# A conditional residual adapter: another order of the opening

## The chip, the cores and the metric

The kernel runs on one core of a Trainium2 chip. The metric is the time of one execution on the device in microseconds. The core has five engines that run side by side, each with its own queue of instructions in program order: TensorE (matmul, PE), VectorE (DVE), ScalarE (ACT), GpSimd (POOL) and SyncE (SP), which here only issues DMAs. Waits between them are semaphores.

## The reference

For each of 128 batches of 128x512 floats an id from 0 to 8 picks one of ten adapters and one of ten rows of gamma, beta and b2:

```python
w1 = W1[language_ids]            # (512, 128) of each batch
w2 = W2[language_ids]            # (128, 512)
h = relu(einsum('bsh,bha->bsa', hidden_states, w1) + b1[language_ids][:, None, :])
adapted = einsum('bsa,bah->bsh', h, w2) + b2[language_ids][:, None, :]
x = hidden_states + adapted
mean = mean(x, axis=-1, keepdims=True)
var = mean(square(x - mean), axis=-1, keepdims=True)
normed = (x - mean) * rsqrt(var + 1e-05)
out = hidden_states + normed * gamma[language_ids][:, None, :] + beta[language_ids][:, None, :]
```

All of it is in float32.

## The kernel before

**Steady work of a batch.** TensorE transposes x in four 128x128 pieces (`transpose_x`, L235), ScalarE copies the result out of PSUM (`copy_xT`, L239), TensorE multiplies by W1 (`down`, L258), ScalarE applies relu and b1 (`relu`, L266), TensorE multiplies by W2 (`up`, L275) into one of five PSUM buffers. VectorE adds the residual and sums the rows (`residual`, L292), ScalarE squares (`square`, L315) and takes the root, VectorE scales by gamma (`scale`, L358) and adds the rest (`finish`, L367). GpSimd prepares two operands ahead of that: x + b2 (`add_b2`, L245) and x + beta (`add_beta`, L252), the latter straight into the output tile. SP stores the outputs of two batches at a time (`store`, L371) from a ring of five output tiles. The loop over `i` works on several batches at once: transposes of batch `i`, `down` of `i - 1`, `up` of `i - 2`, the normalization of `b = i - 3`. The order on every engine is the order in the code; `keep` ties each instruction to the one before it on its engine.

**Where b2 is added.** On GpSimd for most batches. For some, VectorE adds it in PSUM (`b2_by_vector`, L285). For a few, TensorE adds it by one more matmul, a "pick" (`b2_by_matmul`, L274). The choice spreads the load over the three engines.

**The opening.** Gamma, beta and b2 must stand in all 128 partitions, since every batch reads a row by its id. The ten rows of each are loaded into one tile `rows`, split into three bfloat16 parts (L184 to L188), and each of the 30 rows is spread by a matmul with a column of `pick` (`spread`, L206); ScalarE or VectorE copies it out (L209, L211). These 30 turns are interleaved by hand with the transposes and projections of batches 0 to 3. A few matmuls on ones come before (`spin`, L486).

**W1.** The first `FIRST` = 9 batches load their W1 by id from DRAM (`load_first`, L154); each such tile is one of five buffers, so from the sixth on the load waits for the `down` five batches before. Later batches copy it on ScalarE (`stage_w1`, L226) out of one of two resident copies: `w1e` below `EARLY` = 21, in a layout whose x is transposed by strided columns, and `w1` from there on, loaded by four DMAs at i = 8, 10, 12, 14.

**SP's queue** is in the order of the code, too: a DMA whose buffer isn't free holds all behind it. x comes in groups of four batches in four buffers; the loads of the first three groups are split in halves.

Of the kernel before, what the change touches and what calls it, by code (L numbers as in the profile page):

```python
# [8 lines left out]
FP = mybir.dt.float32  # L9
# [7 lines left out]
P = 128  # L17
G = 4
EPS = 1e-5
FIRST = 9  # L20
EARLY = 21
LATE = 12
U = 2

# [2 lines left out]
def cond_resid_kernel(ctx: ExitStack, tc: tile.TileContext, x, itok, W1, b1, W2, b2, gamma, beta, out):  # L27
# [63 lines left out]
    keep(nc.sync.dma_start(out=ids, in_=itok.rearrange("(o b) -> o b", o=1)))  # L91
# [7 lines left out]
    keep(nc.vector.memset(warm, 1.0))  # L99
    keep(nc.scalar.activation(warm, warm, AF.Abs_reciprocal_sqrt))  # L100
    def load_w1(k):
        keep(
            nc.sync.dma_start(out=w1[:, :, k, :], in_=W1[:, k * P : (k + 1) * P, :].rearrange("l p a -> p l a"))
        )

    ident = const.tile([P, P], FP, name="ident")
    make_identity(nc, ident)
    eps = const.tile([P, 1], FP, name="eps")
    nc.gpsimd.memset(eps, EPS)
    ones = const.tile([P, P], BF, name="ones")  # L110
    nc.gpsimd.memset(ones, 1.0)

    R = 3 * L
# [6 lines left out]
    keep(nc.vector.tensor_scalar(pick[:, L : 2 * L], pick[:, L : 2 * L], -0.5, None, ALU.mult))  # L122

    lids, w1s = {}, {}

# [57 lines left out]
    left = rp.tile([P, H], FP, tag="r", name="left")  # L183
    keep(nc.vector.tensor_copy(parts[0:R, :], rows[0:R, :]))  # L184
    keep(nc.vector.tensor_tensor(left[32 : 32 + R, :], rows[0:R, :], parts[0:R, :], ALU.subtract))
    keep(nc.vector.tensor_copy(parts[32 : 32 + R, :], left[32 : 32 + R, :]))
    keep(nc.vector.tensor_tensor(left[64 : 64 + R, :], left[32 : 32 + R, :], parts[32 : 32 + R, :], ALU.subtract))
    keep(nc.vector.tensor_copy(parts[64 : 64 + R, :], left[64 : 64 + R, :]))  # L188

    b1T = const.tile([P, L], FP, name="b1T")  # L190

# [8 lines left out]
    b2_b = const.tile([P, L * H], FP, name="b2_b")  # L200

    def spread(r, copier):
        t = (beta_b, gamma_b, b2_b)[r // L]
        row = p_y.tile([P, H], FP, tag="y", name=f"row_{r}")
        pick_r = pick[:, r : r + 1].to_broadcast([96, P])
        keep(nc.tensor.matmul(row, lhsT=pick_r, rhs=parts[:96, :], start=True, stop=True))  # L206
        dst = t[:, r % L * H : (r % L + 1) * H]
        if copier is nc.scalar:
            keep(nc.scalar.copy(dst, row))  # L209
        else:  # L210
            keep(nc.vector.tensor_copy(dst, row))  # L211
# [56 lines left out]
    def up(b):  # L268
        v = lid(b, ET.PE)
        ys[b] = p_y.tile([P, H], FP, tag="y", name=f"py_{b}")  # L270
        m = b2_by_matmul(b)
        if m:
            pick_b = pick[:, bass.ds(v + 2 * L, 1)].to_broadcast([96, P])
            keep(nc.tensor.matmul(ys[b], lhsT=pick_b, rhs=parts[:96, :], start=True, stop=False))  # L274
        keep(nc.tensor.matmul(ys[b], lhsT=hT[b], rhs=w2[:, bass.ds(v * H, H)], start=not m, stop=True))  # L275
        del hT[b]
# [217 lines left out]

    def spread_turn(lo, hi):
        for r in range(lo, hi):
            spread(r, nc.scalar if r % 7 in (1, 3, 5) else nc.vector)

    def x_turn(b):
        transpose_x(b)  # L500
        copy_xT(b)

    x_turn(0)
    transpose_b1()
    spread_turn(0, 4)
    x_turn(1)
    spread_turn(4, 11)
    down(0)
    relu(0)
    spread_turn(11, 15)  # L510
    down(1)
    relu(1)
    x_turn(2)
    spread_turn(15, 19)
    x_turn(3)
    down(2)
    relu(2)
    spread_turn(19, 24)
    down(3)
    relu(3)  # L520
    spread_turn(24, R)
    up(0)
    up(1)

    for i in range(3, B + U):
        b = i - U - 1
        if b > G and b % G == 2 and b // G + 3 < NG:
            load_x(b // G + 3)
        if i == 5:
            load_x(3)  # L530
        if i in (8, 10, 12, 14):
            load_w1((i - 8) // 2)
        if i == 4:
            up(2)
        if i == 5:
            up(3)
        if i > 3 and on(i):
            transpose_x(i)
        if b <= E:
            add_b2(b + 2)  # L540
            add_beta(b)
        if i > 4 and on(i - 1):
            down(i - 1)
        if i > 3 and on(i):
            copy_xT(i)
        if b == 2:
            scalar_means(0)
            deviation(0)
        if i > 4 and on(i - 1):
            relu(i - 1)  # L550
        if i + 1 >= LATE and on(i + 1):
            stage_w1(i + 1)
        if i > 5 and on(i - U):
            up(i - U)


        g, half = divmod(b, 2)
        p = g - 1
        mine, old = 0 <= p < B // 2, 0 <= p - 1 < B // 2
        if b == E:  # L560
# [36 lines left out]

        for n, engine in ((i + 3, ET.Activation), (i - U + 3, ET.PE), (b + 1, ET.DVE), (b + 5, ET.Pool)):
            if on(n):
                lid(n, engine)  # L600

# [36 lines left out]
```

## Time and profile before

| what | value |
|---|---|
| time, median of 3 runs | 307.37 us (307.01 to 307.51) |
| the profiled execution | 307.08 us |
| its span, first to last instruction | 305.3 us |
| mean granted TensorE clock | 0.991 |
| busy: PE, DVE, ACT, POOL | 294.6, 295.5, 282.1, 283.7 us |
| DMA traffic | 77.85 MB, mean 255 GB/s |

"Busy" is the time in which an engine executes; registers, branches and DMA issues don't count. In the lines of a view "x8" is a number of instructions, and the time after "<-" in brackets is an idle time and what ended it. The chain of waits is followed back from the last instruction, at each step to what released it. A row of stages gives, in order, its length, the busy time of PE, PEld (weight loads), DVE, ACT and POOL with their instructions, the granted clock, the share of the DMA engines and GB/s.

### The profile page before, as it was taken

How to read it: one execution, taken by the hardware profiler on the slowest of the kernel's cores; microseconds unless marked ns; L12 is line 12 of the kernel's file. 1: busy time of each engine (PE TensorE's matmuls, PEld its weight loads, DVE VectorE, ACT ScalarE, POOL GpSimd, SP SyncE). 2: the span in 40 equal slices, each digit the busy share in tenths (PEclk: the TensorE clock that was granted, in tenths of full speed). 3: DMA queues.
4: the chain of work that ended last, by engine and by line, in shares of the span. 5: the costliest groups of instructions: out<-in, count | busy, mean ns of one | idle time of the engine just before them, and what ended most of it. 6: DMA issues, size and time to landing. Idle time of an engine off the chain costs nothing.

```text
span 305.3 us, 6987 instructions
## 1 busy us (share of the span) xinstructions
PE 294.6 (97%) x1836; PEld 220.2 (72%) x1836; DVE 295.5 (97%) x770; ACT 282.1 (92%) x777; POOL 283.7 (93%) x239
## 2 busy tenths in 40 slices
PE   8999999999999999999999999999999999999980
PEld 3748787777777777777777777777777777777740
DVE  6889999999999999999999999999999999999995
ACT  3758999999999999999999999999999999999982
POOL 1349898999999999999999999999999999999995
PEclk9999999999999999999999999999999999999996
DMA  6999999966678667766877666778766767782244
GB/s 234 393 386 387 373 370 355 375 226 251 212 273 273 232 200 232 244 254 224 275 247 235 223 210 251 254 241 275 258 196 221 237 240 235 275 276 105 112 166 172
DMA packets 44057, 77.85 MB, mean 255 GB/s; under 512 B 1993, under 2 KB 7892, under 8 KB 44018
## 3 DMA queue, kind: packets, MB, share of 16 engines
q1 hardware_dynamic: 43382, 76.84, 72.8%
q10 hardware_dynamic: 636, 0.57, 0.6%
q8 instruction: 15, 0.25, 0.3%
q14 instruction: 24, 0.20, 0.2%
HBM read 43.85 MB, written 33.55 MB: 253 GB/s over the span
## 4 chain that ended last, share of the span: by engine, by line
PE 92%; DVE 5%; issue 1%; ACT 1%; DVEq 0%; POOL 0%; ACTq 0%; POOLq 0%
PE ph L258 36%; PE py L275 34%; PE pxT L235 18%; PE row L206 2%; DVE py L358 2%; PE idle L486 1%; DVE py L292 1%; DVE o L367 1%; DVE b_b L211 0%; ACT n L414 0%; ACT sq L315 0%; ACT sq L400 0%; DVE o L425 0%; ACT w1s L226 0%; DVE rstd L334 0%
## 5 line engine op out<-in xcount | busy, mean ns | idle before, releaser
L252 POOL TENSOR_TENSOR o<-x,beta_b 128x512 f32<-128x512 f32 x128 | 163.7, 1294 | 10.5 <-DVE beta_b L211 9.5
L258 PE MATMUL ph<-xT,w1s 128*128 128x128 f32 x1024 | 135.3, 275 | 0.0
L275 PE MATMUL py<-w,hT 128*128 x256 | 131.1, 595 | 0.5 <-DVE b_b L211 0.5
L245 POOL TENSOR_TENSOR r<-x,b_b 128x512 f32<-128x512 f32 x96 | 124.3, 1295 | 7.1 <-DVE b_b L211 6.2
L258 PEld LDWEIGHTS ph<-xT,w1s 128*128 128x128 f32 x1024 | 124.9, 192 | 1.0 <-ACT hT L266 0.5
L235 PEld LDWEIGHTS pxT<-ident,x 128*128 128x128 f32 x512 | 66.6, 151 | 65.3 <-issue 49.3
L358 DVE SCALAR_TENSOR_TENSOR py<-py,nmean,gamma_b 128x512 f32<-128x512 f32 x126 | 95.2, 755 | 0.2
L367 DVE SCALAR_TENSOR_TENSOR o<-py,rstd,o 128x512 f32<-128x512 f32 x122 | 91.4, 750 | 0.0
L315 ACT ACTIVATE sq<-py,sum 128x512 f32<-128x512 f32 x124 | 85.8, 692 | 2.8 <-DVE py L292 2.6
L235 PE MATMUL pxT<-ident,x 128*128 128x128 f32 x512 | 78.2, 276 | 0.0
L239 ACT COPY xT<-pxT 128x512 f32<-128x512 f32 x128 | 74.7, 583 | 3.6 <-PE pxT L235 3.6
L292 DVE SCALAR_TENSOR_TENSOR py<-py,r 128x512 f32<-128x512 f32 x96 | 66.6, 693 | 0.2
L226 ACT COPY w1s<-w 128x512 f32 x107 | 65.6, 613 | 0.0
L266 ACT ACTIVATE hT<-ph,b1T 128x128 f32<-128x128 f32 x128 | 46.9, 366 | 8.2 <-PE ph L258 2.9
L275 PEld LDWEIGHTS py<-w,hT 128*128 128x128 f32 x256 | 39.2, 192 | 2.7 <-issue 1.0
L315 ACT ACTIVATION_READ_ACCUMULATOR sq<-py,sum 128x1 f32 x124 | 25.1, 202 | 0.0
L292 DVE SCALAR_TENSOR_TENSOR py<-py,x 128x512 f32<-128x512 f32 x32 | 22.4, 699 | 0.4
L285 DVE TENSOR_TENSOR py<-py,b_b 128x512 f32<-128x512 f32 x29 | 20.2, 697 | 0.7 <-PE py L275 0.6
L325 ACT ACTIVATE root<-ssq,eps 128x2 f32<-128x2 f32 x62 | 16.4, 265 | 0.0
L292 DVE DVE_READ_ACCUMULATOR py<-py,r 128x1 f32 x96 | 13.8, 143 | 0.0
L306 ACT ACTIVATE nmean<-sum 128x2 f32<-128x2 f32 x62 | 12.3, 198 | 0.0
L329 DVE SCALAR_TENSOR_TENSOR part<-ssq,root 128x2 f32<-128x2 f32 x62 | 9.4, 152 | 0.2 <-ACT root L325 0.2
(55 smaller groups left out, 92.0 us busy)
## 6 DMA issues: line engine op xcount, KB each, us to landing
out_dram<-o SPq DMA_DIRECT2D x61, 512.0 KB, 3.4
x<-in_x_dram SPq DMA_DIRECT2D x29, 1024.0 KB, 6.6
x<-in_x_dram SPq DMA_DIRECT2D x6, 512.0 KB, 8.7
w1e<-in_L_cond_W_dram SPq DMA_DIRECT2D x2, 1280.0 KB, 12.4
w<-in_L_cond_W_dram SPq DMA_DIRECT2D x4, 640.0 KB, 8.0
w1s<-in_L_cond_W_dram SPq DMA_DIRECT2D x9, 256.0 KB, 8.1
w<-in_L_cond_W_dram SPq DMA_DIRECT2D x1, 1792.0 KB, 10.0
w<-in_L_cond_W_dram SPq DMA_DIRECT2D x1, 768.0 KB, 5.3
```

The lines of the kernel that those rows point to most:

```text
L226: keep(nc.scalar.copy(w1s[b].rearrange("p k a -> p (k a)"), src))
L235: keep(nc.tensor.transpose(pxs[b][:, k, :], cols, ident))
L239: keep(nc.scalar.copy(xT[b], pxs.pop(b)))
L245: keep(nc.gpsimd.tensor_tensor(rs[b], xb(b), b2_b[:, bass.ds(v * H, H)], ALU.add))
L252: keep(nc.gpsimd.tensor_tensor(os[g][:, j, :], xb(b), beta_b[:, bass.ds(v * H, H)], ALU.add))
L258: nc.tensor.matmul(phs[b], lhsT=w1s[b][:, k, :], rhs=xT[b][:, k, :], start=(k == 0), stop=(k == KC - 1))
L266: keep(nc.scalar.activation(hT[b], phs.pop(b), AF.Relu, bias=b1T[:, bass.ds(lid(b, ET.Activation), 1)]))
L275: keep(nc.tensor.matmul(ys[b], lhsT=hT[b], rhs=w2[:, bass.ds(v * H, H)], start=not m, stop=True))
L292: nc.vector.scalar_tensor_tensor(ys[b], ys[b], 1.0, r, ALU.mult, ALU.add, accum_out=col(sums, b))
L315: nc.scalar.activation(sq, ys[b], AF.Square, bias=col(sums, b), scale=-float(H), accum_out=col(ssqs, b))
L358: nc.vector.scalar_tensor_tensor(ys[b], ys[b], col(nmeans, b), gamma_b[:, bass.ds(v * H, H)], ALU.add, ALU.mult)
L367: nc.vector.scalar_tensor_tensor(o, ys.pop(b), rstds[g][:, j : j + 1], o, ALU.mult, ALU.add)
```

## The change

The opening is written anew.

- **Loads.** Gamma and b2 go to `rows`, b1 follows, and beta goes four times into a zeroed tile `beta_rows`, once at the head of each 32 partitions. x of batches 0, 1, 2 and 3 is loaded one batch at a time. W2 comes in halves of five, behind the W1 of batch 2. The fourth group of x (`x_3`) is loaded ahead of the loop.
- **Rows.** Only gamma and b2 are spread by picks (20 turns, R = 20). Beta's rows are spread by ten VectorE shuffles (`beta_row`). The three bfloat16 parts are made by two subtractions on VectorE and two copies on ScalarE, which read the upper halves of the floats.
- **b2** of batches 0 to 3, 14 and 18 is added by TensorE; batch 5's goes to GpSimd.
- **W1** is loaded by id for 12 batches instead of 9; `w1e` serves up to batch 29 instead of 20, and the loads of `w1` move to i = 16, 18, 20, 22.
- **Order.** Batch 3's transposes and `down` move behind the first `up`. `add_beta` runs two batches earlier in GpSimd's order, next to `add_b2` of the same batch. The spin loses a half matmul.

```diff
-FIRST = 9
-EARLY = 21
+FIRST = 12
+EARLY = 30
...
-    keep(nc.scalar.dma_start(out=rows[0:L, :], in_=beta))
-    keep(nc.sync.dma_start(out=rows[L : 2 * L, :], in_=gamma))
-    keep(nc.scalar.dma_start(out=rows[2 * L : 3 * L, :], in_=b2))
-    load_part(0, 2)
-    keep(nc.scalar.dma_start(out=b1r, in_=b1))
+    beta_rows = rp.tile([P, H], FP, tag="r", name="beta_rows")
+    keep(nc.vector.memset(beta_rows, 0.0))
...
+    def load_beta(q, engine):
+        keep(engine.dma_start(out=beta_rows[32 * q : 32 * q + L, :], in_=beta))
...
+    keep(nc.scalar.dma_start(out=rows[0:L, :], in_=gamma))
+    keep(nc.sync.dma_start(out=rows[L : 2 * L, :], in_=b2))
+    keep(nc.scalar.dma_start(out=b1r, in_=b1))
+    load_beta(0, nc.scalar)
+    load_beta(1, nc.sync)
+    load_beta(2, nc.scalar)
+    load_beta(3, nc.sync)
+    load_part(0, 1)
+    load_part(1, 2)
...
-    load_w2(0, 3)
     load_first(0)
     load_first(1)
-    load_part(2, G)
+    load_part(2, 3)
     load_first(2)
+    load_w2(0, 5)
+    load_w2(5, L)
+    load_part(3, G)
     load_first(3)
-    load_w2(3, L)
...
     load_part(2 * G, 2 * G + 2)
+    load_first(2 * G)
     load_early(0, 5)
-    load_first(2 * G)
+    load_first(2 * G + 1)
+    load_part(2 * G + 2, 3 * G)
+    load_first(2 * G + 2)
     load_early(5, L)
-    load_part(2 * G + 2, 3 * G)
+    load_first(2 * G + 3)
+    xs[3] = xp.tile([P, G, H], FP, tag="x", name="x_3")
+    load_part(3 * G, 3 * G + 2)
+    load_part(3 * G + 2, 4 * G)
...
+    keep(nc.vector.tensor_tensor(rows[32 : 32 + R, :], rows[0:R, :], upper(0), ALU.subtract))
+    keep(nc.scalar.copy(parts[0:R, :], upper(0)))
+    keep(nc.vector.tensor_tensor(parts[64 : 64 + R, :], rows[32 : 32 + R, :], upper(32), ALU.subtract))
+    keep(nc.scalar.copy(parts[32 : 32 + R, :], upper(32)))
...
-        return b in (5, B - 2, B - 1)
+        return b < 4 or b in (14, 18) or b >= B - 2
...
-        return b < 4 or 8 <= b < B - 8 and (b % 4 == 1 if b < 24 else b % 16 in (1, 6, 11) or b % 32 == 30)
+        return 8 <= b < B - 8 and (b % 4 == 1 if b < 24 else b % 16 in (1, 6, 11) or b % 32 == 30)
...
     spin(9, H)
-    spin(1, H // 2)
...
+    def beta_row(lo, hi):
+        for r in range(lo, hi):
+            keep(nc.vector.stream_shuffle(beta_b[:, r * H : (r + 1) * H], beta_rows, [r] * 32))
...
+    transpose_b1()
+    beta_row(0, 3)
     x_turn(0)
+    spread_by(S_, 0)
+    spread_by(V, 1)
+    spread_by(S_, 2)
+    spread_by(V, 3)
     x_turn(1)
     down(0)
     relu(0)
+    spread_by(S_, 4)
+    x_turn(2)
+    spread_by(S_, 5)
+    spread_by(V, 6)
     down(1)
     relu(1)
+    beta_row(3, 5)
...
     down(2)
     relu(2)
...
+    spread_by(V, 14)
+    beta_row(5, 7)
+    spread_by(S_, 15)
+    spread_by(S_, 16)
+    spread_by(S_, 17)
+    spread_by(V, 18)
+    spread_by(S_, 19)
+    up(0)
+    beta_row(7, 10)
+    add_beta(0)
+    add_beta(1)
+    add_beta(2)
+    add_beta(3)
+    x_turn(3)
+    up(1)
     down(3)
     relu(3)
...
-        if i in (8, 10, 12, 14):
-            load_w1((i - 8) // 2)
+        if i in (16, 18, 20, 22):
+            load_w1((i - 16) // 2)
...
             add_b2(b + 2)
-            add_beta(b)
+            if 4 <= b + 2 <= E:
+                add_beta(b + 2)
...
-        if 0 < g and b <= E and half == 1:
+        if 0 <= g and b <= E and half == 1:
             scalar_means(g)
             deviation(g)
```

More of the change, by code (lines that the diff above doesn't have):

```diff
@@ L104, in load_w1 @@
         )
+    ones = const.tile([P, P], BF, name="ones")
+    nc.gpsimd.memset(ones, 1.0)
     ident = const.tile([P, P], FP, name="ident")
@@ L109, in cond_resid_kernel @@
     nc.gpsimd.memset(eps, EPS)
-    ones = const.tile([P, P], BF, name="ones")
-    nc.gpsimd.memset(ones, 1.0)
-    R = 3 * L
+    R = 2 * L
     parts = const.tile([P, H], BF, name="parts")
@@ L121, in cond_resid_kernel @@
     keep(nc.vector.tensor_tensor(pick, both, ident[:96, 64 : 64 + R], ALU.add))
-    keep(nc.vector.tensor_scalar(pick[:, L : 2 * L], pick[:, L : 2 * L], -0.5, None, ALU.mult))
+    keep(nc.vector.tensor_scalar(pick[:, 0:L], pick[:, 0:L], -0.5, None, ALU.mult))
     lids, w1s = {}, {}
@@ L177, in cond_resid_kernel, with upper @@
     load_part(2 * G, 2 * G + 2)
+    load_first(2 * G)
     load_early(0, 5)
-    load_first(2 * G)
+    load_first(2 * G + 1)
+    load_part(2 * G + 2, 3 * G)
+    load_first(2 * G + 2)
     load_early(5, L)
-    load_part(2 * G + 2, 3 * G)
[L183 to L188, printed above, removed]
+    load_first(2 * G + 3)
+    xs[3] = xp.tile([P, G, H], FP, tag="x", name="x_3")
+    load_part(3 * G, 3 * G + 2)
+    load_part(3 * G + 2, 4 * G)
+    def upper(lo):
+        return rows[lo : lo + R, :].bitcast(BF)[:, 1 : 2 * H : 2]
+    keep(nc.vector.tensor_tensor(rows[32 : 32 + R, :], rows[0:R, :], upper(0), ALU.subtract))
+    keep(nc.scalar.copy(parts[0:R, :], upper(0)))
+    keep(nc.vector.tensor_tensor(parts[64 : 64 + R, :], rows[32 : 32 + R, :], upper(32), ALU.subtract))
+    keep(nc.scalar.copy(parts[32 : 32 + R, :], upper(32)))
     b1T = const.tile([P, L], FP, name="b1T")
@@ L202, in spread @@
     def spread(r, copier):
-        t = (beta_b, gamma_b, b2_b)[r // L]
+        t = (gamma_b, b2_b)[r // L]
         row = p_y.tile([P, H], FP, tag="y", name=f"row_{r}")
@@ L272, in up @@
         if m:
-            pick_b = pick[:, bass.ds(v + 2 * L, 1)].to_broadcast([96, P])
+            pick_b = pick[:, bass.ds(v + L, 1)].to_broadcast([96, P])
             keep(nc.tensor.matmul(ys[b], lhsT=pick_b, rhs=parts[:96, :], start=True, stop=False))
@@ L492, in cond_resid_kernel @@
     spin(9, H)
-    spin(1, H // 2)
     def spread_turn(lo, hi):
         for r in range(lo, hi):
-            spread(r, nc.scalar if r % 7 in (1, 3, 5) else nc.vector)
+            spread(r, nc.vector if r >= L and r % 2 else nc.scalar)
     def x_turn(b):
@@ L501, in x_turn, with spread_by @@
         copy_xT(b)
+    def beta_row(lo, hi):
+        for r in range(lo, hi):
+            keep(nc.vector.stream_shuffle(beta_b[:, r * H : (r + 1) * H], beta_rows, [r] * 32))
+    def spread_by(copier, *rows_):
+        for r in rows_:
+            spread(r, copier)
+    V, S_ = nc.vector, nc.scalar
+    transpose_b1()
+    beta_row(0, 3)
     x_turn(0)
-    transpose_b1()
-    spread_turn(0, 4)
+    spread_by(S_, 0)
+    spread_by(V, 1)
+    spread_by(S_, 2)
+    spread_by(V, 3)
     x_turn(1)
-    spread_turn(4, 11)
     down(0)
     relu(0)
-    spread_turn(11, 15)
+    spread_by(S_, 4)
+    x_turn(2)
+    spread_by(S_, 5)
+    spread_by(V, 6)
     down(1)
     relu(1)
-    x_turn(2)
-    spread_turn(15, 19)
-    x_turn(3)
+    beta_row(3, 5)
+    spread_by(S_, 7)
+    spread_by(S_, 8)
+    spread_by(V, 9)
     down(2)
     relu(2)
-    spread_turn(19, 24)
+    spread_by(S_, 10)
+    spread_by(V, 11)
+    spread_by(S_, 12)
+    spread_by(S_, 13)
+    spread_by(V, 14)
[13 more added lines that the diff above has]
+    up(1)
     down(3)
     relu(3)
-    spread_turn(24, R)
-    up(0)
-    up(1)
     for i in range(3, B + U):
@@ L528, in cond_resid_kernel @@
             load_x(b // G + 3)
-        if i == 5:
-            load_x(3)
-        if i in (8, 10, 12, 14):
-            load_w1((i - 8) // 2)
+        if i in (16, 18, 20, 22):
+            load_w1((i - 16) // 2)
         if i == 4:
@@ L545, in cond_resid_kernel @@
             copy_xT(i)
-        if b == 2:
-            scalar_means(0)
-            deviation(0)
         if i > 4 and on(i - 1):
@@ L596, in cond_resid_kernel @@
             stage_w1(i + 1)
-        for n, engine in ((i + 3, ET.Activation), (i - U + 3, ET.PE), (b + 1, ET.DVE), (b + 5, ET.Pool)):
+        for n, engine in ((i + 3, ET.Activation), (i - U + 3, ET.PE), (b + 1, ET.DVE), (b + 6, ET.Pool)):
             if on(n):
```

2 lines of the change are left out of this document (1 added, 1 removed).

## The prediction

> **What bounds the kernel now.** I read the page's busy shares first, then the stages, then the waits, and at the opening the chain and the order of time.
>
> ```profile
> PE 294.6 (97%) x1836; PEld 220.2 (72%) x1836; DVE 295.5 (97%) x770; ACT 282.1 (92%) x777; POOL 283.7 (93%) x239
> ```
>
> ```profile
> 18.00:24.00 6.00, 5.54 (x23) 2.94 (x21) 5.30 (x11) 3.32 (x9) 4.32 (x4) 1.00 1.05 387
> 24.00:60.00 36.00, 36.00 (x230) 28.49 (x229) 35.73 (x94) 33.96 (x97) 34.11 (x29) 1.00 1.07 372
> 60.00:280.00 220.00, 220.00 (x1403) 166.81 (x1402) 219.64 (x574) 215.29 (x602) 220.00 (x179) 1.00 0.70 239
> ```
>
> From 24 us on TensorE never rests (220.00 of 220.00), and VectorE and GpSimd are as full: three engines share one beat. The DMA engines are full until 60 us (share 1.07, 372 to 387 GB/s), then at 0.70.
>
> ```profile
> 54.43 0.89 PE ph L258 x8
> 55.32 0.86 PE py L275 x2
> 56.18 0.47 PE pxT L235 x4
> 56.65 0.89 PE ph L258 x8
> 57.54 0.86 PE py L275 x2
> 58.40 0.44 PE pxT L235 x4
> ```
>
> The chain of waits shows the beat: 0.89 + 0.86 + 0.47 = 2.22 us per batch while transposes read columns with a stride, 2.19 from the batch (21) on which they don't. So the end is the opening, plus TensorE's work, plus a tail that I leave alone. The opening, again from the chain and the waits:
>
> ```profile
> 17.66 1.30 DVE b_b L211 x2
> 18.96 2.81 PE py L275 x6
> ```
>
> ```profile
> POOL o L252 <- DVE beta_b L211: 9.5, 1, 9.5
> POOL r L245 <- DVE b_b L211: 6.2, 1, 6.2
> ```
>
> The first up projection starts at 18.96, after VectorE copied the last picked rows; GpSimd, without slack later, does two additions and then stands until b2 is spread (19.68).
>
> **The change part by part.** Everything is against the profiled execution: 307.08 us, 0.29 under the median 307.37.
>
> *Loads up to W2.* The row for W2's 1792 KB load says 10.0 us to landing; issued at 6.05, it lands at 16.05, with 4673 KB in the queue up to it. Now 4222 KB lead to W2's end: four copies of beta (+60 KB), less of x and two W1 blocks fewer. At 387 GB/s (378 KB/us) that is 1.2 us less. Against it, batch 0's x is issued some 0.7 us later (two beta loads at 0.3 to 0.4 on SP go ahead), which leaves the queue about 0.36 us behind. W2: 16.05 - 1.2 + 0.36 = 15.2. Batch 0's x lands near 5, as now (4.8 by the queue).
>
> *Parts.* Three casts (0.41) and two subtractions (0.68) on VectorE become two subtractions and two ScalarE copies. ScalarE now issues four DMAs (0.3 each more) before its table load, which ends near 3.7; copies of 0.41 (cast row) to 0.61 (L226 row) give parts at 5.1 instead of 5.88. TensorE is then with batch 0's transposes: nothing gained or lost. The missing half spin and the zeroing of the beta tile (twice the 0.27 of the memset of half its size, so 0.5 on VectorE) lie before 5 us, ahead of the loads that they could delay only by the 0.2 counted above.
>
> *Spreading.* Thirty picked rows become twenty: 13 copies on ScalarE (0.53 apart), 7 on VectorE (0.64), ten shuffles on VectorE. No shuffle is in the trace. Below it lies a memset-like 0.27 to 0.5, above it GpSimd's 1.29 for the same 128x512; nearest are VectorE's 0.64 copy and its 0.70 tensor_tensor, so I take 0.65. [...] ScalarE up to row 15's copy: 3 copies of xT (0.58), 10 rows (0.53), 3 relus (0.3), 7.9 us from 6.5, so 14.4 with no wait. TensorE's last row is freed by VectorE's copy of row 14: seven slots more of 0.65 from 5.6, with waits for TensorE, about 14.3; in the trace 0.8 us pass between the last row's issue (18.1) and the first up projection, in which TensorE's sequencer reads ids. So 15.1 by rows, 15.2 by W2, and I take **15.6** for a few handovers: 3.36 earlier.
>
> *TensorE's work behind that point.* Batch 3's transposes (0.47) and down projection (0.89) move from before to behind, and b2 for batches 0 to 3 adds four picks of 0.22 (the beat with batch 5's pick is 2.44 against 2.22): +2.24. The stretch from 18.96 to batch 6's down projection at 27.57 takes 8.61 for 7.92 of work; of its 0.69 of waiting, mostly transposes waiting on ScalarE's copy, I take half back, since VectorE's four b2 additions (0.70 each) are gone and ScalarE's squares come sooner: -0.34. Batch 5's pick goes: -0.22. At batch 8 TensorE is then 3.36 - 2.24 + 0.34 + 0.22 = **1.68 ahead**.
>
> *GpSimd and VectorE follow?* The last shuffle stands behind rows 14 and 18 on VectorE: near 18.1. GpSimd then does thirteen additions at 1.235 to batch 8's residual: 34.2, wanted at 36.32 - 1.68 = 34.6. It holds by 0.4; now it has 6.7 there. This cover is what the change spends. ScalarE's three dropped W1 copies (0.61) are off the path.
>
> *Loads behind W2.* SP's queue now halts at W1 blocks 8 to 11, each waiting for the down projection five earlier; behind it queue the copy of W1, batches 10 to 15 and the first store. The engines still have work, since the backlog at each halt is over 3 us. GpSimd got batch 10's x at
>
> ```profile
> 32.98 1.28 POOL L245 TENSOR_TENSOR r<-x,b_b 128x512 f32<-128x512 f32 x1 [0.94 <-DMA x<-in_x_dram]
> ```
>
> with 10561 KB in the queue up to it. Batch 12's x now ends 11902 KB: 32.9 + 1341/378 + 0.36 = 36.8. TensorE transposed it at 38.26 and would want it at 36.58: **+0.35** with its handover. The first store ends 12926 KB, 39.5; beta's addition for batch 10, now two batches earlier in GpSimd's order, needs that output buffer and would be due at 37.9. Three additions later batch 12's residual is ready at 44.6, wanted at 43.95: VectorE is late by 0.6, which the five-deep PSUM ring about covers.
>
> *Later.* Picks for batches 14 and 18: +0.44. Nine more strided batches at 2.22 instead of 2.19: +0.27. Loads of w1 move to 16, 18, 20, 22, due at batch 30; no cost.
>
> Sum: -1.68 + 0.35 + 0.44 + 0.27 = -0.62, 306.46 for the profiled run and **306.7** at the median. About 0.2% (0.61 us) is what a measurement here can tell from no change, so below 306.76 is faster and above 307.98 slower: this stands at the edge.
>
> **Rivals.**
> 1. *x of batch 12 in time.* If the queue starts no later, x lands at 36.4 and TensorE keeps its 1.68 (or 2.0, if all the waiting goes): 306.0 to 306.4. For: TensorE's start here is bound by handovers, not loads. Against: the DMA share is 1.05 from 6 us on, so every KB counts.
> 2. *The output ring.* If the first store lands 0.8 us later than worked out (behind 12926 KB the sixteen engines may be apart), batch 12's residual is 1.4 late, the ring covers 0.6, and 0.8 is lost: 307.5. For: GpSimd waits for a store once in the trace, 0.8 us, in the crowded stage. Decides: GpSimd standing for over 2.2 us ahead of beta's addition.
> 3. *Dear shuffles.* At 1.1 each the last five alone, with waits, put GpSimd's start near 21; batch 8's residual then comes at 37.1, 0.8 after its present 36.32, and with 0.5 of ring and 0.71 of later work the kernel ends 1.0 to 1.5 slower: 308.6. Decides: a start of GpSimd after 19.6. Against: the nearest rows are 0.64 and 0.70.
> 4. *TensorE at half speed for longer.* The order of time shows ten spins in 4.45 us, 0.43 each for 512 columns, and rows of the same width at 0.22 after 6.6; batch 0's transposes take 1.06 instead of 0.63. If nine spins leave a gap and full speed comes 3 us later, TensorE loses 1.5 of a stretch with almost no slack (9.0 of work from 5.4 to 14.5): 308.2. Against: the gap is under 0.4. [...]
> 5. *Spreading no shorter.* Handovers between the two copiers hold the first up projection to 17: 1.4 late, 308.1, slower or the same.
>
> **How the numbers follow.** Forecast 0.42 (its own range 306.2 to 307.2; 0.34 of it faster, 0.08 within), rival 1: 0.14, all faster; rival 2: 0.18 (0.15 within, 0.03 slower); rival 3: 0.11 slower; rival 4: 0.05 (0.04 slower); rival 5: 0.10 (half each). Faster 0.48, within 0.29, slower 0.23. The range runs from rival 1 to rival 3, 305.9 to 308.6, and leaves out dearer shuffles and a gain of all waiting.
>
> **What would show it.** Right: W2 landing near 15.2, first up projection near 15.6, GpSimd's start near 18.1, batch 8's down projection (32.23 now) near 30.6, a short wait of TensorE for x near 36.6, the 2.19 beat untouched behind batch 30. Wrong: shuffles over 0.8; GpSimd starting after 19; a wait for a store over 2.2 us; an up projection after 17; or a beat behind batch 30 other than 2.19, for then the opening is not what sets the end.

## The result

| | median | range | runs |
|---|---|---|---|
| before | 307.35 us | 306.87 to 307.55 | 15 |
| after | 309.42 us | 307.76 to 311.97 | 15 |

The ratio is 1.0068 (1.0044 to 1.0091): the change makes the kernel slower. The forecast was 306.7, with a range up to 308.6. The runs after spread over 4 us where those before spread over 0.7, and the mean granted clock goes with it: the six runs up to 308.49 have 0.989 to 0.994, the nine from 309.36 on 0.979 to 0.988. One execution of b4_before_w2_late below took 1759.32 us, for a reason that the record doesn't show, and its row counts the other nine.

The profiled execution took 311.97 us (span 310.2, clock 0.980) against 307.08. It is the slowest of the fifteen: the median is 2.07 us above the median before, the profiled execution 4.89 above the profiled one before. The busy line of the page after:

```profile
PE 296.4 (96%) x1830; PEld 222.0 (72%) x1830; DVE 292.9 (94%) x774; ACT 281.7 (91%) x776; POOL 282.4 (91%) x238
```

The stages after; behind the length come PE, PEld, DVE, ACT and POOL, then the granted clock, the DMA share and GB/s:

```profile
6.00:12.00 6.00, 4.42 (x31) 3.39 (x29) 3.22 (x8) 3.61 (x8) 0.00 (x0) 1.00 0.94 272
12.00:18.00 6.00, 4.39 (x22) 2.05 (x20) 5.61 (x15) 5.10 (x11) 0.00 (x0) 1.00 1.05 398
18.00:24.00 6.00, 5.20 (x11) 2.90 (x12) 2.00 (x6) 0.59 (x1) 4.75 (x4) 0.50 1.05 387
24.00:60.00 36.00, 36.00 (x226) 28.68 (x225) 32.09 (x83) 30.90 (x87) 31.28 (x27) 0.99 0.94 336
60.00:280.00 220.00, 220.00 (x1402) 167.62 (x1401) 219.55 (x573) 214.73 (x601) 219.22 (x179) 1.00 0.74 251
```

Three readings. From 6 to 12 us the DMA engines move 272 GB/s, though they are nearly always taken (0.94); the same row of the kernel before reads

```profile
6.00:12.00 6.00, 6.00 (x38) 4.02 (x37) 5.08 (x9) 4.64 (x9) 1.01 (x1) 1.00 1.04 393
```

From 18 to 24 us TensorE has half its clock (0.50; 1.00 before) and gets 11 instructions done where it did 23. And behind 24 us TensorE never rests again, as before. The chain of waits after, in order of time (start, length, what):

```profile
6.25 12.42 DMA w<-in_L_cond_W_dram
18.67 0.14 issue
18.80 2.05 PE py L294 x2
20.85 0.85 PE pxT L254 x4
21.70 0.43 PE py L293
22.13 1.71 PE py L294 x2
23.84 1.44 PE ph L277 x8
```

W2's second half takes 12.42 us from its issue and ends at 18.67, not 15.2; the first up projection (L294) starts at 18.80. Then the pieces take about twice their usual time: 2.05 for two matmuls that take 0.86, 0.85 for transposes that take 0.47, 1.44 for a down projection of 0.89, in whose course full speed comes back. The records of the granted clock hold half speed from 18.03 to 24.86. TensorE's waits and the first two of GpSimd's:

```profile
PE py L294 <- DMA w<-in_L_cond_W_dram: 2.1, 1, 2.1
PE pxT L254 <- DMA x<-in_x_dram: 1.2, 1, 1.2
```

```profile
POOL o L271 <- DVE beta_b L523: 17.8, 1, 17.8
POOL o L271 <- DMA out_dram<-o: 5.4, 2, 4.7
```

GpSimd starts at 19.25 where it was to start at 18.1. It later stands 4.7 us for a store, but TensorE has no wait to show for that.

Laid side by side from the starts of TensorE's instructions:

| stretch | before | after | difference |
|---|---|---|---|
| to the first up projection | 18.96 | 18.80 | -0.16 |
| from there to batch 8's down | 13.11 | 17.69 | +4.58 |
| to batch 30's down | 48.52 | 49.22 | +0.70 |
| to the last up projection | 215.17 | 215.14 | -0.03 |
| to the end of the span | 9.54 | 9.35 | -0.19 |

All of the 4.9 us arises between 18 and 86 us, and nearly all of it before batch 8.

### The profile page after: what moved, and what is told of

Its sections match the earlier page's. It is cut to its first block, busy times and chain, and to the rows that moved or that the text cites. A ratio compares the mean times of both kernels' runs of the same rounds, so it can differ in the third digit from the quotient of the medians.

```text
span 310.2 us, 7027 instructions
## 1 busy us (share of the span) xinstructions
PE 296.4 (96%) x1830; PEld 222.0 (72%) x1830; DVE 292.9 (94%) x774; ACT 281.7 (91%) x776; POOL 282.4 (91%) x238
## 4 chain that ended last, share of the span: by engine, by line
PE 89%; DMA 4%; DVE 3%; ACT 1%; issue 1%; SPq 1%; DVEq 0%; ACTq 0%
PE ph L277 36%; PE py L294 35%; PE pxT L254 18%; DMA w<-in_L_cond_W_dram 4%; DVE py L377 1%; DVE py L311 0%; PE py L293 0%; SPq L164 0%; ACT n L433 0%; DVE rows L204 0%; ACT sq L334 0%; ACT sq L419 0%; DVE o L444 0%; DVE o L386 0%; ACT w1s L245 0%
## 5 line engine op out<-in xcount | busy, mean ns | idle before, releaser
L294 PE MATMUL py<-w,hT 128*128 x256 | 133.3, 603 | 2.1 <-DMA w<-in_L_cond_W_dram 2.1
L264 POOL TENSOR_TENSOR r<-x,b_b 128x512 f32<-128x512 f32 x95 | 122.9, 1294 | 0.0
L254 PEld LDWEIGHTS pxT<-ident,x 128*128 128x128 f32 x512 | 67.9, 155 | 66.6 <-issue 50.0
L311 DVE SCALAR_TENSOR_TENSOR py<-py,r 128x512 f32<-128x512 f32 x95 | 65.5, 690 | 1.4 <-PE py L294 0.5
L245 ACT COPY w1s<-w 128x512 f32 x98 | 60.0, 613 | 0.0
L294 PEld LDWEIGHTS py<-w,hT 128*128 128x128 f32 x256 | 39.8, 194 | 3.5 <-issue 2.4
L304 DVE TENSOR_TENSOR py<-py,b_b 128x512 f32<-128x512 f32 x25 | 17.3, 691 | 0.1
L344 ACT ACTIVATE root<-ssq,eps 128x2 f32<-128x2 f32 x62 | 16.5, 265 | 0.0
L245 ACT COPY w1s<-w1e 128x512 f32 x18 | 11.0, 610 | 0.0
```

Of the source, the lines that this page charges most:

```text
L245: keep(nc.scalar.copy(w1s[b].rearrange("p k a -> p (k a)"), src))
L254: keep(nc.tensor.transpose(pxs[b][:, k, :], cols, ident))
L264: keep(nc.gpsimd.tensor_tensor(rs[b], xb(b), b2_b[:, bass.ds(v * H, H)], ALU.add))
L311: nc.vector.scalar_tensor_tensor(ys[b], ys[b], 1.0, r, ALU.mult, ALU.add, accum_out=col(sums, b))
```

## The experiments

The letters in the expectations: L is W2 landing late, C is the clock that falls in the wait for it, S is SP's halts behind W2, N is chance; A puts the slow stretch of the queue down to the four loads of beta, D to a queue that runs dry while SP waits for the ids, B to the 256 KB blocks themselves; G is GpSimd's late start, T another cause for the end. The first table is for all of them: W2's end, the first up projection and batch 8's down in the profiled execution, the DMA rate from 6 to 12 us, and the ratio to the kernel before on the same chip. In the profiled executions of after, a1, a3, b1, c2 and d3 the clock fell ahead of batch 8, which is in their last two columns.

| run | median us | ratio | GB/s | W2 | first up | batch 8 |
|---|---|---|---|---|---|---|
| before | 307.35 | | 393 | 16.05 | 18.96 | 32.07 |
| after | 309.42 | 1.0068 (1.0044 to 1.0091) | 272 | 18.67 | 18.80 | 36.49 |
| a1_again | 310.76 | 1.0111 (1.0081 to 1.0141) | 274 | 18.30 | 18.44 | 34.83 |
| a2_warm | 308.92 | 1.0041 (1.0028 to 1.0055) | 284 | 18.12 | 18.26 | 33.01 |
| a3_w2_first | 310.63 | 1.0107 (1.0076 to 1.0138) | 355 | 17.21 | 20.12 | 34.86 |
| a4_batch3_ahead | 308.89 | 1.0056 (1.0036 to 1.0075) | 300 | 19.16 | 19.29 | 32.68 |
| b1_beta_once | 309.25 | 1.0048 (1.0026 to 1.0070) | 281 | 17.65 | 17.78 | 34.18 |
| b2_x_bridge | 309.74 | 1.0067 (1.0036 to 1.0097) | 297 | 17.79 | 17.93 | 32.68 |
| b3_bridge_batch3 | 308.18 | 1.0023 (1.0008 to 1.0039) | 313 | 18.13 | 18.17 | 31.58 |
| b4_before_w2_late | 309.42 | 1.0050 (1.0033 to 1.0067) | 291 | 18.23 | 18.84 | 31.94 |
| c1_old_order | 307.87 | 1.0030 (1.0014 to 1.0046) | 370 | 16.98 | 17.63 | 32.30 |
| c2_opening_only | 308.84 | 1.0050 (1.0037 to 1.0063) | 369 | 16.81 | 19.01 | 33.69 |
| c3_opening_batch3 | 309.88 | 1.0090 (1.0074 to 1.0107) | 372 | 16.88 | 18.83 | 32.14 |
| d1_no_ids | 309.12 | 1.0067 (1.0051 to 1.0084) | 318 | 16.75 | 16.88 | 31.63 |
| d2_opening_picks | 308.61 | 1.0057 (1.0035 to 1.0078) | 374 | 16.89 | 18.84 | 32.15 |
| d3_beta_first | 308.29 | 1.0041 (1.0024 to 1.0059) | 374 | 17.39 | 19.54 | 34.29 |

### The same kernel again, and with the clock held

a1_again is the changed kernel without an edit. a2_warm puts nine spins where TensorE waits for W2:

```diff
     spread_by(S_, 19)
+    spin(9, H)
     up(0)
```

> The changed kernel as it is, for a second profile. In the first, W2 landed at 18.7 us (forecast 15.2), TensorE stood for 2.1 us before the first up projection, and the granted clock was 0.50 from 18 to 24 us. Theory C (clock): TensorE's light load while it waits for W2 lets the granted clock fall to one half, and that costs about 3 us; whether it falls depends on the run, so this run shows it or not, and the time goes with the mean granted clock: 311 to 312 us at 0.980, near 308.3 at 0.990 or above. Theory L (loads): W2 is late in each run, since the DMA queue runs dry near 5 us while SP waits for the ids, and packets after that are slow; W2 lands at 17.5 to 19 here too. Rival N (chance): the first profile was an odd one, W2 lands near 15.5 here, and the time is near 307.5.

> Nine idle matmuls of 512 columns (1.95 us at full clock) after the last spread row, before the first up projection, so that TensorE has work while W2 comes. Theory C: the granted clock stays at 1.00 from 18 to 24 us, the time is 307.8 to 308.6 and its spread over the runs shrinks to under 1 us. Theory L alone: W2 still lands at 17.5 to 19, the matmuls fit into the wait, and without a part for the clock the time stays at 309 to 310. If W2 comes at 15.5, the matmuls cost up to 1.9 us and the time is 309 or more.

a1_again lost its clock too, for one stretch (18.73 to 22.15; 0.72 in the row from 18 to 24 us), and is again slower. In a2_warm the clock stays full from 4.26 to 301 us. Its row of the stage and the head of its chain:

```profile
18.00:24.00 6.00, 5.74 (x27) 3.81 (x27) 2.86 (x7) 2.19 (x6) 5.33 (x5) 1.00 1.05 386
```

```profile
6.24 11.88 DMA w<-in_L_cond_W_dram
18.12 0.14 issue
18.26 1.10 PE py L294 x2
```

The first up projection is nearly as late as without the spins (18.26, against 18.80 and 18.44), but it takes 1.10 and not 2.05, and from it to batch 8 it is 14.75 us instead of 17.69: the clock costs 2.94 of the profiled execution after, and 1.64 of that of a1 (16.39), which had one stretch of half speed. None of the eight runs is below 0.989. W2 late is untouched by that, and with it the kernel stays 0.4% slower. So two causes, and one hangs on the other. Two things were expected and did not come: the median is 0.3 above the range, and the runs still spread over 1.45 us (308.09 to 309.54), though their clocks agree within 0.005 (309.36 has 0.994). So the clock isn't all that spreads the runs.

### W2 ahead, and batch 3 ahead

```diff
 a3_w2_first
+    load_w2(0, 3)
     load_first(0)
     load_first(1)
     load_part(2, 3)
     load_first(2)
-    load_w2(0, 5)
-    load_w2(5, L)
+    load_w2(3, L)
```

```diff
 a4_batch3_ahead
     load_first(2)
+    load_part(3, G)
+    load_first(3)
     load_w2(0, 5)
     load_w2(5, L)
...
+    x_turn(3)
     beta_row(5, 7)
...
     spread_by(S_, 16)
+    down(3)
+    relu(3)
```

> Three of W2's ten rows (768 KB) are loaded right behind x of batch 1, ahead of the first load by id, the other seven where the two halves stood; the bytes up to W2's end are the same. Theory L: the queue no longer runs dry near 5 us, the packets stay near 84 ns, W2 lands at 15.2 to 16, and the time falls to 306.8 to 307.8 although the first down projection comes some 2 us later. Theory C alone: nothing changes in W2's lateness if the dry queue is not its cause; W2 at 18 to 19 and 309 to 310 us as in the changed kernel.

> Batch 3's transposes and down projection go back ahead of the first up projection (behind row 14 and row 16), and the loads of batch 3's x and W1 ahead of W2. Theory S (SP's halts): the load of batch 8's W1 block, which waits for batch 3's down projection, and all behind it go out 6 us sooner, the DMA engines no longer idle from 24 to 28 us, and TensorE has 1.4 us of work in what was waiting: 307.5 to 308.5. Theory C: the same work in the wait keeps the clock up in most runs, 308 to 309. Theory L alone: W2 lands 1.4 us later still (512 KB more ahead of it) and the time is 310 or more.

W2 first ends at 17.21, 1.1 to 1.5 earlier, but the first block of W1 then comes at 10.52; TensorE stands for it, loses its clock from 11.85 to 15.26 (0.73 in the row from 12 to 18 us), and the last picked row is issued at 19.25. What one load gains the other pays, and the 306.8 to 307.8 that were expected became 310.63. Batch 3 ahead lets W2 come still later (19.16) and yet is no slower than the change (the intervals of the two ratios overlap): TensorE has work in the wait, and batch 8's block, which waits for batch 3's down projection, is issued at 19.28 and not at 25.30. The clock stays full in its profile; three of its seven runs have 0.985 to 0.987 and are the three slowest.

### What slows the queue from 5 to 12 us

```diff
 b1_beta_once
-    load_beta(1, nc.sync)
-    load_beta(2, nc.scalar)
-    load_beta(3, nc.sync)
```

```diff
 b2_x_bridge
+    load_part(2, G)
     load_first(0)
     load_first(1)
-    load_part(2, 3)
     load_first(2)
     load_w2(0, 5)
     load_w2(5, L)
-    load_part(3, G)
     load_first(3)
```

b3_bridge_batch3 is b2_x_bridge with batch 3's work moved as in a4_batch3_ahead and `load_first(3)` ahead of W2. b4 is an edit of the kernel before:

```diff
 b4_before_w2_late
-    load_w2(0, 3)
     load_first(0)
     load_first(1)
     load_part(2, G)
     load_first(2)
+    load_w2(0, 3)
     load_first(3)
```

> The changed kernel with one load of beta instead of four (the other three groups of 32 partitions keep the zeros of the memset, so three quarters of beta_b are left out; no instruction of an engine changes). Theory A (the four loads of beta hold up SP and ScalarE and spoil the queue: the 2 KB packets of 0.2 to 1.9 us between 5 and 12 us come from them): the ids' loads and W1's first block are issued 0.3 us earlier, packets are back at 84 ns, the DMA engines move 380 GB/s and more between 5 and 12 us, W2 is complete by 15.5, the first up projection begins by 16.5, and the time falls to 307.5 or below. Theory D (the queue runs dry while SP waits for the ids, and the packets suffer from the restart whatever went before): 250 to 260 GB/s between 5 and 12 us as before, W2 complete at 18 or later, time 308.5 to 311 as the changed kernel.

> The changed kernel with x of batches 2 and 3 (512 KB) issued right behind x of batch 1, ahead of the first W1 block that is loaded by its id, so that the queue has 1.3 us more in it while SP waits for the ids. W2 then has 256 KB more ahead of it, 0.7 us. Theory D (dry queue): no dry moment near 5 us, 350 GB/s or more between 5 and 12 us, W2 complete by 16.5 in spite of the 256 KB, first up projection near 17, time 307 to 308. Theory A (the loads of beta): 260 GB/s stays, W2 complete near 19, time 309 to 311.

> The kernel with batch 3's transposes, down projection and relu back ahead of the first up projection (as the earlier run with batch 3 ahead, 308.89) and with x of batches 2 and 3 issued ahead of the first block by id. W2 has 512 KB more ahead of it than in the changed kernel, 1.35 us. Theory D: packets at 84 ns, W2 complete at 16.5 to 17, first up projection at 17 to 17.5, TensorE 1.6 ahead of the kernel before at batch 8 minus 0.9 for the picks; with 0.5 for later picks and strides the time is 306.8 to 307.4. Theory A: W2 complete at 19 as in that earlier run, time 308.5 to 309.3. Theory C (what is left is the clock): the clock stays full behind 6 us in both, so it decides nothing here.

> The kernel before with its first three rows of W2 (768 KB) moved from ahead of the W1 blocks that wait for the ids to behind the third of them, as the changed kernel has it; the bytes up to W2's end are the same. Theory D: between the end of x of batches 0 and 1 (near 5 us) and the first block by id the queue runs dry, packets of 0.2 us and more appear between 5 and 12 us, 300 GB/s or less there, W2 complete 1.5 to 3 later than 16.05, and the time rises by 1 to 2.5. Theory A (the loads of beta do it): no such packets, W2 complete within 0.5 of 16.05, time within 0.3 of the kernel before.

Three loads of beta fewer (b1, which leaves three quarters of beta's rows at zero): 281 GB/s, little better. More x in the queue: 297 and, in b3, 313, with W2 at 17.79 and 18.13; theory D had expected 350 and more, and W2 by 16.5 to 17. But the kernel before, with one load moved, drops from 393:

```profile
6.00:12.00 6.00, 6.00 (x39) 4.12 (x38) 5.20 (x10) 4.64 (x9) 1.13 (x1) 1.00 0.87 291
```

The order of the loads alone does that in the kernel before, without a load of beta changed, and A falls. b4 shows something more. Its first up projection (18.84) and batch 8 (31.94) are not later than in the kernel before, since picked rows set them there. It loses its 2 us afterwards: the whole queue is 2.2 us late, the early copy of W1 ends at 33.73 instead of 31.51, and ScalarE has a wait that the kernel before hasn't:

```profile
ACT w1s L226 <- DMA w1e<-in_L_cond_W_dram: 1.7, 1, 1.7
```

b3_bridge_batch3 is the only edit of these whose runs all keep the clock (0.989 to 0.993, 307.56 to 308.84). It is 0.49 ahead of the kernel before at batch 8 and 0.58 behind it at batch 30.

### The old order of loads, with and without the rest

```diff
 c1_old_order
-    load_beta(0, nc.scalar)
-    load_beta(1, nc.sync)
-    load_beta(2, nc.scalar)
-    load_beta(3, nc.sync)
-    load_part(0, 1)
-    load_part(1, 2)
+    load_part(0, 2)
+    for q in range(4):
+        load_beta(q, nc.scalar)
...
+    load_w2(0, 3)
     load_first(0)
     load_first(1)
-    load_part(2, 3)
+    load_part(2, G)
     load_first(2)
-    load_w2(0, 5)
-    load_w2(5, L)
-    load_part(3, G)
     load_first(3)
+    load_w2(3, L)
```

c2_opening_only goes on from c1: FIRST 9, EARLY 21, the loads behind W2 and `load_w1` as in the kernel before, and no picks for 14 and 18. c3_opening_batch3 is c2 with batch 3's work ahead.

> The changed kernel with the loads up to W2 in the order of the kernel before: x of batches 0 and 1 in one load of 512 KB as SP's third, the first three rows of W2 (768 KB) right behind it, then the blocks by id; the four loads of beta all on ScalarE's queue. Everything else as changed. Theory D (W2 was late because loads of 256 KB that SP can issue only behind the ids stood where those 1280 KB stood, so the engines idled and packets were slow between 5 and 12 us): 370 GB/s or more there, W2 complete at 16.0 to 16.5 (4733 KB against 4673), first up projection at 16.3 to 16.8, the clock full from 7 us on, TensorE 0.5 to 0.9 ahead of the kernel before at batch 8; with 0.71 for the later picks and strides the time is 306.9 to 307.7. Theory A (the loads of beta, or something of the changed program, whatever the order): 250 to 300 GB/s stays, W2 at 18 or later, time 308.5 to 310.

> As the run with the old order, and behind W2 everything as in the kernel before too: nine blocks by id, the early copy of W1 up to batch 20, W1's loads at 8 to 14, x of batches 12 to 15 in one load, no picks for batches 14 and 18. What is left of the change is the opening on the engines: twenty picked rows, shuffles, b2 of batches 0 to 3 on TensorE. Theory D with the prediction's later terms (0.44 for picks, 0.27 for strides): 0.7 faster than the run with the old order, 306.2 to 306.9, TensorE 0.5 to 0.9 ahead at batch 8 and at batch 30. Theory S (behind W2 the queue is as full as before, so that being earlier only meets x of batch 10 or W1's copy): the lead is gone by batch 12 with a wait of TensorE or GpSimd for a load, time within 0.3 of the kernel before.

> As the run with the opening only, with batch 3's transposes, down projection and relu ahead of the last picked rows, as the kernel before has them. It tells whether work moved behind the first up projection is a cost of its own or only a question of order. If TensorE has no rest either way (theory D), both are within 0.3 of each other at batch 8 and in time; if TensorE stands before the first up projection in the run with the opening only (W2 later than 16.5), this one is 0.3 to 1.0 faster than it, 306 to 306.6.

With c1 the rate is back:

```profile
6.00:12.00 6.00, 4.12 (x25) 2.85 (x24) 3.17 (x8) 3.06 (x7) 0.00 (x0) 1.00 1.03 370
```

The very blocks by id that were slow after land 0.68 us apart here (8.85, 9.53), at 256 KB a rate of 385 GB/s; B falls as well. W2 is complete at 16.98. But now beta's loads, queued on ScalarE behind x, land up to 8.42, W1's first block at 8.85, and the chain goes through the copies of the picked rows:

```profile
15.09 1.46 ACT b_b L224 x3
16.54 0.04 issue
16.59 0.59 PE row L221 x2
17.18 0.23 issue
17.41 0.38 PE py L289
17.79 0.86 PE py L290 x2
```

The first up projection comes at 17.63, 1.3 ahead of the kernel before, and at batch 8 TensorE is 0.23 behind it. The time, 307.87, is 0.2 over the expected range and no gain. The runs of c1 also show the price of the clock by itself: seven lie at 307.74 to 307.96 (0.989 to 0.993), three at 309.33 to 309.52 (0.984). The gap of 1.7 us is half of the 3.41 us that the profiles of a3 and d3 have at half speed, and a1 and b1, each with one such stretch behind the first up projection (0.72 in the row from 18 to 24 us of both), need 1.64 and 1.65 more to batch 8 than a2.

c2 misses its expectation, and so does c3. From batch 8 to batch 30 c2 takes 48.51 us, as the kernel before (48.52), so the 0.71 for picks and strides is real. But from the last up projection to the end c2 and c3 take 11.1 us where the kernel before takes 9.5. The chain of the kernel before runs near its end through VectorE and ScalarE, that of c3 through GpSimd. Two cuts, the kernel before first:

```profile
298.19 0.76 DVE py L358
300.36 0.67 DVE py L358
301.20 0.48 DVE o L425
```

```profile
293.97 4.91 POOL o L261 x4
298.88 1.22 POOL n L425
300.19 1.25 POOL o L427
301.45 1.22 POOL n L425
```

with waits for GpSimd's x + b2 that the kernel before hasn't:

```profile
DVE py L301 <- POOL r L254: 2.8, 8, 0.6
```

GpSimd starts at 21.30 here and not at 10.99. By 21.30 it had done 4.12 us of additions in the kernel before, and batch 5's b2 is one more here. It is busy for 283.54 of the 283.70 us from there to 305, so it never makes that up: more than 270 us later it ends the kernel.

### The ids taken away, the picks given back, beta ahead

```diff
 d1_no_ids
-        src = W1[bass.ds(lid(b, ET.SP), 1)]...
+        src = W1[bass.ds(lid(b, ET.SP), 1) if b > 2 else slice(0, 1)]...
```

```diff
 d2_opening_picks (from c3)
-        return b < 4 or b >= B - 2
+        return b < 4 or b in (14, 18) or b >= B - 2
```

d3_beta_first is c1 with the four loads of beta ahead of `load_part(0, 2)`, two on ScalarE and two on SP.

> The changed kernel, in which the first three blocks of W1 that are loaded by id are loaded from language 0, so that SP need not wait for the ids before it issues them (the output of batches 0 to 2 is that of another language's W1; bytes, order and instructions of the engines are the same). Theory D (SP issues these loads late and one by one, so the queue is nearly empty): they are issued by 4 us, the DMA engines move 370 GB/s or more between 5 and 12 us, W2 is complete at 15.2 to 15.8 as the prediction had it, the first up projection begins at 16.0 to 16.5 (behind the last picked row, 15.5, and not at 15.6), TensorE is 1.0 to 1.4 ahead of the kernel before at batch 8 (16.26 instead of 15.6 in the prediction's sum), x of batch 12 costs 0.3 to 0.6, and the time is 306.9 to 307.5. Theory B (blocks of 256 KB are slow there whoever issues them): 250 to 310 GB/s stays, W2 at 17.5 or later, time 308.5 or more.

> The run with the opening and batch 3 ahead (309.88), and the two picks for batches 14 and 18 back. Theory G (GpSimd starts 10 us later than in the kernel before and, as full as the beat, never makes that up; behind the last up projection, 9.5 us before the end in the kernel before, its backlog costs 1.6): two additions less, 2.5 us of GpSimd's time, bring the stretch behind the last up projection back to 9.3 to 9.6, TensorE loses 0.44 less what it waited between batches 12 and 16 (0.63), and the time falls to 307.7 to 308.5. Theory T (the longer stretch at the end has another cause): the stretch stays at 11.1 and the time goes to 310 or more.

> The run with the old order (307.87), with the four loads of beta ahead of x of batches 0 and 1, two on SP and two on ScalarE, as the changed kernel has them. In the old-order run VectorE stood 3.1 us for the beta rows and ScalarE 3.3 us. If that set its first up projection (17.63): it comes at 16.9 to 17.2 now, TensorE is 0.2 to 0.6 ahead of the kernel before at batch 8, and the time is 307.1 to 307.6. If W2 (16.98 there) and x, each 0.5 us later for two more issues of SP, set it: first up projection at 17.5 or later and 307.8 to 308.3.

In d1 the blocks are issued from 3.17 to 4.59 instead of 3.85 to 5.39. The rate from 6 to 12 us rises, but only to 318, and W2 is complete at 16.75: 1.5 to 1.9 earlier than in the two profiles of the changed kernel, still 1.5 later than forecast. The rate lies between what theories D and B expected: SP's wait for the ids is a part of it, not all.

```profile
5.54 11.21 DMA w<-in_L_cond_W_dram
16.75 0.14 issue
16.88 1.10 PE py L294 x2
```

W2 still ends the wait. From there the forecast's own chain holds: 14.75 us to batch 8 (14.79 by the prediction's terms), 0.44 ahead there, 0.47 for x of batch 12, 0.74 behind at batch 30. The profiled execution took 308.14, and the median 309.12 misses the expected 307.5.

d2 takes two additions from GpSimd, and the stretch behind the last up projection goes from 11.1 to 9.9, the median from 309.88 to 308.61: GpSimd's late start is shown, though 0.3 more was expected of the stretch and 0.1 of the time. The picks for 14 and 18 are thus no extra of the change but the price of the late start. In d3 beta lands by 3.8 and W1's blocks 0.4 later than in c1; the profiled execution lost its clock from 11.24 to 14.65 (0.94 in the row from 6 to 12 us, 0.78 in the next) in a wait for them, and its five quickest runs, 308.00 to 308.32, are at their middle 0.4 slower than c1's seven quickest. None of these kernels is faster than the one before.

## Why the prediction was wrong

**The step that failed first: W2 at 15.2.** The sum divided 4222 KB by a rate of 378 KB/us taken from the full queue of the kernel before. The change replaces the 1280 KB that kept that queue full, x in one load and a first part of W2, by loads of 256 KB, three of which SP can issue only behind the ids. There the rate was 272 GB/s, and W2 came 3.5 late. An estimate from the rows splits the 3.5 us in three. From 6 to 12 us 121 GB/s are missing, at 387 GB/s 1.9 us. Up to 6 us the queue had moved 139 GB/s instead of 191, 0.8 us, of which the sum had allowed 0.36. And the trace has sixteen signals for the landing of a load, as many as the core has DMA engines: for W2's second half thirteen had come by 17.28, the last three only from 18.17 to 18.67, 1.4 us more. The lag of three is in its first half, too (13.90, then 14.79 to 15.29). Together that is 3.7; 398 GB/s from 12 to 18 us gives 0.2 back. In a2 and d1 the last three are within 0.4 us of the thirteenth.

That the slow stretch comes and goes with the order of the loads is shown in both kernels (b4, c1; c1 also loads x in bigger pieces, b4 changes the order alone). Why the queue is that slow there is not shown: from 5 to 12 us 60 of 953 packets take over 0.2 us, up to 1.9, instead of 84 ns (1 of 1429 in the kernel before), but in b4, hardly faster, only 15 of 1059 do; and filling the queue with x (b2) or issuing the blocks early (d1) mends it by 25 to 46 GB/s of the 121 missing.

**Rival 4 had the mechanism, at another place.** It feared the clock ahead of batch 0, and there nothing happened: full speed began at 4.38 us, and at 6.49 in the kernel before. But a late W2 leaves TensorE with little work: behind the last picked rows, up to 16.11, it had a rest of 0.23, one pick of 0.38 and then 2.08 of waiting. Full speed ended at 18.03, with 1.31 of the 2.08 us gone, and came back after 6.83 us; in the 3.41 us up to 18.03 TensorE was busy for 1.77. No run shows the 3 us by which the rival lets full speed come later, the author's estimate; the stretches at half speed in such waits took 6.83 us (after), 3.42 (a1) and 3.41 (a3, d3). That the work in the wait matters is shown by a2, which only adds nine spins there: its clock is 1.00 from 18 to 24 us, and none of its eight runs is below 0.989, where nine of the fifteen runs after are at 0.988 or less.

How little work loses the clock is not shown. In the row of 6 us, of those behind 6 us, in which TensorE has least work it is busy for 2.64 us (a3), 3.84 (d3) and 3.98 (c2) from 6 to 12, and for 4.07 (a1), 4.33 (b1) and 4.39 (after) from 12 to 18, and the clock falls in that row or in the next. It stays at 1.00 in both with 3.92 (c3), 4.12 (c1), 4.15 (d2), 4.29 (b3) and 4.45 (a4) from 6 to 12 and with 4.39 (b2) and 4.80 (d1) from 12 to 18. So the busy time of such a row doesn't decide: b2 kept its clock with the 4.39 with which the changed kernel lost it.

**A cover that wasn't there.** That "the backlog at each halt is over 3 us" was wrong: batch 8's block waits for batch 3's down projection, which the change puts behind the first up projection. The block was issued at 25.30, and the queue had run out by then; that is in the 336 GB/s of the stage to 60 us (372 before). From 24.86 to 28.27 it moves 135 GB/s. As TensorE was later still, it cost nothing that a wait of TensorE shows. Rival 2's sign, GpSimd standing over 2.2 us for a store, appeared (4.7) without its price, for the same reason.

**What held.** The parts were ready at 5.1 as forecast. Shuffles, taken at 0.65, start 0.62 to 0.64 apart where nothing stands between them:

```profile
17.21 0.70 DVE L523 STREAM_SHUFFLE beta_b<-beta_rows 128x512 f32<-128x512 f32 x1
17.83 0.71 DVE L523 STREAM_SHUFFLE beta_b<-beta_rows 128x512 f32<-128x512 f32 x1
```

The last picked row was issued at 15.73 after, 15.42 in a1 and 15.02 in d1, 2.4 to 3.1 earlier than before (18.12): spreading was shorter, and rivals 3 and 5 did not decide. It was still 0.7 to 1.4 later than the 14.3 of the sum, so with W2 in time the first pick for batch 0, issued at 16.34 after and 15.63 in d1, would have missed the 15.6 in the one and met it in the other. Work behind the first up projection, 14.79 us by the terms +2.24, -0.34 and -0.22, took 14.75 in a2, b2 and d1; that is partly luck, since the first of the four picks runs ahead of it and the terms without that pick give 14.57. The wait for x of batch 12, taken at 0.35, was 0.56 in a2, 0.36 in b3, 0.47 in d1 and only 0.12 in b2. Picks and strides, 0.71, cost 0.70. The beat of 2.19 stood in every kernel. One slip in the prediction changes no sum: one W1 block and one batch of x fewer lead to W2's end, not two blocks (4222 KB is right).

**The sum made again.** -0.62, with +3.20 for the first up projection at 18.80 instead of 15.6, +2.94 for the clock, -0.35 for a wait that a late TensorE doesn't have, and -0.19 at the end, is +4.98; the profiled execution is 4.89 longer. The same terms say what the change would have needed: 1.64 of work behind the first up projection (14.75 against 13.11) and 0.70 later must be won ahead of it, so a first up projection by 16.6, or by 16.1 with the 0.47 that d1 waits for x of batch 12. The earliest of all profiles, with the ids taken away, had 16.88. The moved work was no saving: ten picked rows fewer bought time on VectorE and ScalarE, and what was late next was the queue.

**What stays open**: the cause of the slow queue and of the lag of three signals, and how W2's end varies between executions that weren't profiled; the six runs of the changed kernel below 308.5 will have had it earlier, or the clock kept, or both, which no profile shows.

## What to carry to other kernels

A rate read from a full queue holds only while the queue is full (393 GB/s from 6 to 12 us before, 272 after): when a change cuts the loads ahead of the one that matters into pieces, or puts an address read ahead of them, work out the backlog at each issue before dividing bytes by the rate. A wait of TensorE can cost more than its length when the matmuls around it are few: here the wait for W2 took the clock too, and that cost 2.94 us in the profile after and 1.64 in a1, for 6.83 and 3.42 us at half speed. Look at the granted clock around such a wait before pricing it. And where an engine is as full as the beat, as GpSimd in c3 (busy for 283.54 of 283.70 us), a late start of it is not made up; look for it in the chain at the far end of the kernel.

## What the runs showed that was not expected

- Half speed lasted 6.83 us in the profile after, 3.42 in a1's and 3.41 in those of a3 and d3, and one stretch of the shorter kind cost a busy TensorE 1.64 (a1) and 1.65 us (b1); c1's times fall into two groups just that far apart.
- In the profile after, the clock was lost 1.31 us into a rest, with TensorE busy for 1.77 of the 3.41 us up to there; nine spins in the wait kept it (1.00 in every row of a2's profile, and 0.989 to 0.994 in its eight runs). The busy time of a row of 6 us doesn't tell the two cases apart: 4.39 in both after and b2, with 0.50 in the next row of the one and 1.00 in that of the other.
- The same 256 KB loads move at 385 GB/s behind a load of 768 KB (c1), and the queue at 291 from 6 to 12 us when that load is moved behind them (b4). In the changed kernel three of the sixteen signals of W2's landing came 0.9 to 1.4 us behind the thirteenth, for its first half and for its second.
